# Causal attention on one core: scores are centred and transposed before the exponential, and rows are divided per token

## The chip, the cores and the metric

The kernel runs on one core of one Trainium2 chip. The metric is the device time of one execution in microseconds (us): 4361.49 us, median of 3 runs (4361.11 to 4366.51). Engines: PE is TensorE (matmuls and transposes), DVE VectorE, ACT ScalarE, POOL GpSimd, SP the engine that issues the DMAs.

## The reference, cut to what matters

Three kinds of layer follow each other over 8 batches of 512 tokens by 256 features. The change touches only the last attention, "attention b":

```python
qkv = x @ w_qkv + b_qkv                     # 16 heads of 16
dot = einsum('bhid,bhjd->bhij', q, k)
vals = q_norm_sq + k_norm_sq.T
scores = dot * dot / (vals - 2.0 * dot + 1e-6)
scores = scores + triu(ones, k=1) * -1e9     # causal
attn = softmax(scores, axis=-1)
out = einsum('bhij,bhjd->bhid', attn, v)
return out @ w_out + b_out
```

Everything is float32. The batches are worked through in two groups of four; in each group attention a, a feed-forward block x, attention b and a feed-forward block y follow each other, so attention b stands twice in the program.

## The kernel before, in words

**Units and steps.** In attention b a batch is cut into four row blocks of 128 queries, i = 0 to 3; block i sees 128(i+1) keys. A unit is what fits into two PSUM banks: 2 x 4 heads of 128 keys for i = 0, 2 x 2 heads of 256 for i = 1, 2 x 1 heads of 384 for i = 2 (768 columns in all), 2 x 1 heads of 512 for i = 3 (1024 columns, as for i = 0 and 1). So a batch has 2 + 4 + 8 + 8 = 22 units and a group 88. The two halves of a unit are called a = 0 and a = 1. `steps` runs a software pipeline by hand: in step s, unit s gets its denominators, unit s-1 its squares, unit s-2 its maximum, unit s-3 is transposed, and in odd steps units s-5 and s-4 are multiplied with the values. `order_keeper` ties every instruction of an engine to the one issued before it on that engine, so the order in which the parts stand in `each_part` is the order on each engine; engines meet only by semaphores.

**What a unit does.** `product` makes den (the denominator, 18 rows) and, a step later, dot (16 rows) on PE, line L1312; the matmuls of den(s) and dot(s-1) take turns. `inverse` is a logarithm and an exponential on ACT (both recorded under the helper's line L241, tile r). `error` (L1331, tile t, reads den and r) and `refine` (L1335) improve 1/den on DVE. `squares` (L1341) squares dot on ACT into num, ahead of `inverse` in the step where the unit has several heads in a half (i = 0 and 1), after it otherwise. `masked` (L1347) adds the mask on POOL. `highest` (L1354) multiplies num by r and keeps each head's row maximum, one DVE instruction for a head; POOL negates it (L1364). `exponentials` (L241, num from num) is one ACT instruction for a head, with the maximum as bias and the row sum as a second output. `turn` (L1384) transposes one half, block by block of 128, into the single PSUM buffer of pool `ps_mm`; `keep_turned` (L1389) copies it to SBUF on DVE. `values` (L1399) multiplies with v.

**Buffers.** Pool `ps_s` has three PSUM buffers of two banks and is used by den, dot and one piece per step; `ps_mm` and `ps_o` (the sums over values) have one each.

**Pieces.** Work beside the units is cut into pieces with up to five parts (`first`, `act`, `second`, `dve`, `late`) that `each_part` puts at fixed places of a step. `stacks_and_values` gives the 11 pieces that prepare the next batch: one transpose, eight side pieces (called heavy: two matmuls `pu`, a square on ACT `sq` (L1210), a matmul with `sel_b` as the part `second` (L1213), an eviction on DVE (L1226) or ACT (L1232)), and two value pieces `pv`. `project` gives two pieces per row block, that divide and project the finished rows. `a_piece` chooses one piece for a step: projections first where the step is odd or their number is even, then a preparing piece, but no heavy one in an odd step beyond the fourth; if there is none, an idle matmul `kept_awake` (L1289). What is left of the preparation when the next batch begins is run by `whole`, part after part, ahead of that step:

```python
if step % each == 0:
    with kept_order():
        while prologues or norms:
            whole((norms or prologues).popleft())
```

Of the kernel before, what the change touches and what calls it, by code (L numbers as in the profile page):

```python
# [11 lines left out]
F32 = mybir.dt.float32  # L12
# [28 lines left out]
Unit = namedtuple("Unit", "n product inverse error refine masks squares masked highest exponentials turn keep_turned values project")  # L41
# [5 lines left out]
def kernel(  # L47
# [14 lines left out]
    b_wo,  # L62
    f_wqkv,
# [108 lines left out]
    def weights_b(name):  # L172
        flat = wts.tile([P, 4096], F32, tag="wa", name=f"wb_{name}", bufs=2)
        wl, at = part(flat, 0, (2, INNER))
        wr, at = part(flat, at, (2, INNER))
        wv, at = part(flat, at, (2, D))
        wo, at = part(flat, at, (4, D))
        bv, at = part(flat, at, (D,))
        for s, d in ((b_wl, wl), (b_wr, wr), (b_wv, wv), (b_wo, wo)):
            fetch(s, d)  # L180
        fetch(b_bv, bv, False)
        return wl, wr, wv, wo, bv
# [991 lines left out]
    def attention_b(batches, g, norms_b, state):  # L1174
        wl_b, wr_b, wv_b, wo_b, bv_b = weights_b(g)

        def stacks_and_values(b):
# [72 lines left out]
            def value_piece(t2):  # L1250
# [13 lines left out]
                def keep_values():  # L1264
                    if t2 == 0:
                        state[b]["v"] = pool.tile([P, NT, (HB + 1) * HDB], F32, tag="v", name=f"v_b{b}")
                        nc.gpsimd.memset(state[b]["v"][:, :, HB * HDB :], 1.0)
                    pv = got.pop("pv")
                    for i in range(2):
                        nc.vector.tensor_add(state[b]["v"][:, 2 * t2 + i, : HB * HDB], pv[:, i, 0], bv_b)  # L1270
# [22 lines left out]
        def unit(b, i, qp, js, first, last):  # L1293
# [55 lines left out]
            def highest(num, r):  # L1349
# [14 lines left out]
                nc.gpsimd.tensor_scalar(most[:, 8 : 8 + nh], most[:, :nh], -1.0, 0.0, ALU.mult, ALU.add)  # L1364
                return most

            def exponentials(num, most):
                if first:
                    state["sums"] = pool.tile([P, HB], F32, tag="sumsb", name=f"sums_{n}")
                sums, s4 = state["sums"], per_head(num)  # L1370
                for at, (a, m, h) in enumerate(heads):
                    function(
                        s4[:, a, m, :],
                        s4[:, a, m, :],
                        AF.Exp,
                        bias=most[:, 8 + at : 9 + at],
                        accum_out=sums[:, h : h + 1],
                    )
                return sums

            def turn(p, a):
                ppt = ps_mm.tile([P, NT, P], F32, tag="mm", name=f"ppt_{n}_{a}")
                for k in range(cols // P):
                    nc.tensor.transpose(ppt[:, k, :], p[:, a, k * P : (k + 1) * P], ident)  # L1384
                return ppt

            def keep_turned(ppt, pt, a):
                nblocks = cols // P
                nc.vector.tensor_copy(pt[:, a, :nblocks, :], ppt[:, :nblocks, :])  # L1389

            def values(pt):
# [3 lines left out]
                v = state[b]["v"]  # L1395

                def one(m, j, k, a):
# [3 lines left out]
                        lhsT=v[:, k, (4 * j + q) * HDB : (4 * j + q + 2) * HDB],  # L1401
# [12 lines left out]
            def project(sums):  # L1414
# [5 lines left out]
                nc.vector.reciprocal(sums, sums)  # L1420

                def turned():
                    prt = ps_s.tile([P, 2, 4, P], F32, tag="s", name=f"prt_{n}")
                    for k in range(4):
                        for q in range(4):
                            one = sums[:, 4 * k + q : 4 * k + q + 1].to_broadcast([P, 32])
                            nc.tensor.matmul(
                                prt[q * 32 : (q + 1) * 32, 0, k, :], lhsT=one, rhs=ident, start=True, stop=True
                            )
                    kept_awake(prt)  # L1430
                    got["prt"] = prt[:, 0]

                def kept():
                    got["rt"] = pool.tile([P, 4, P], F32, tag="two", name=f"rt_{n}", bufs=7)
                    nc.scalar.copy(got["rt"], got.pop("prt"))

                def divided():
                    got["oT"] = pool.tile([P, 4, P], F32, tag="two", name=f"oT_{n}", bufs=7)
                    nc.vector.tensor_mul(got["oT"], state["o"], got.pop("rt"))

                def projected():
                    got["pp"] = ps_s.tile([P, 2, T], F32, tag="s", name=f"pp_{n}")[:, 0, :D]
                    for k in range(4):
                        nc.tensor.matmul(
                            got["pp"], lhsT=got["oT"][:, k, :], rhs=wo_b[:, k, :], start=(k == 0), stop=(k == 3)
                        )

                def added():
                    nc.vector.tensor_add(xs[b][:, i, :], got.pop("pp"), xs[b][:, i, :])

                return [Piece(False, turned, kept, None, divided), Piece(False, projected, None, None, added)]

            return Unit(n, product, inverse, error, refine, len(js), squares, masked, highest, exponentials, turn, keep_turned, values, project)
# [9 lines left out]
        def steps(ahead):  # L1463
# [6 lines left out]
            den, dot, r, t, num, most, sums, ppt, pt = ({} for _ in range(9))  # L1470
# [18 lines left out]
            def each_part(s):  # L1489
# [5 lines left out]
                with_values = s % 2 == 1 and unit_of(5) is not None  # L1495
                if with_values:
                    for u in (s - 5, s - 4):
                        projections.extend(units[u].project(sums.pop(u)))
                piece = a_piece(s) if s >= EARLY_STEPS else Piece(False)
# [4 lines left out]

                products = []
# [8 lines left out]
                if unit_of(3):  # L1514
                    pt[s - 3] = pool.tile([P, 2, NT, P], F32, tag="pt", name=f"pt_{units[s - 3].n}", bufs=3)
                    turned = units[s - 3].turn(num[s - 3], 0)
                do(piece.first)
                if with_values:
                    in_turns(*[units[u].values(pt.pop(u)) for u in (s - 5, s - 4)])
                if unit_of(1):  # L1520
                    units[s - 1].refine(t.pop(s - 1), r[s - 1])

# [3 lines left out]
                if unit_of(0):  # L1526
                    r[s] = units[s].inverse(den[s])
                do(piece.act)
                if unit_of(1) and not first:
                    num[s - 1] = units[s - 1].squares(dot.pop(s - 1))  # L1530
                if unit_of(2):
                    most[s - 2] = units[s - 2].highest(num[s - 2], r.pop(s - 2))
                if unit_of(1):
                    units[s - 1].masked(num[s - 1])
                if unit_of(3):
                    units[s - 3].keep_turned(turned, pt[s - 3], 0)
                    turned = units[s - 3].turn(num.pop(s - 3), 1)
                do(piece.second)
                if unit_of(2):
                    sums[s - 2] = units[s - 2].exponentials(num[s - 2], most.pop(s - 2))  # L1540
                if unit_of(0):
                    t[s] = units[s].error(den.pop(s), r[s])
                if unit_of(3):
                    units[s - 3].keep_turned(turned, pt[s - 3], 1)
# [96 lines left out]
def laid_out(inputs):  # L1641
# [18 lines left out]
    wo_b = np.zeros((HB, 2, HDB, D), f)  # L1660
    wo_b[:, 0] = i["L0_attn_b_w_out"].reshape(HB, HDB, D)
    wo_b[HB - 1, 1, 0] = i["L0_attn_b_b_out"]

# [4 lines left out]
    for half, rest in ((0, 0), (1, GATES)):  # L1668
# [19 lines left out]
        "b_wo": wo_b.reshape(INNER, D),  # L1688
# [28 lines left out]
```

## Time and profile before

| | |
|---|---|
| median of 3 runs | 4361.49 us |
| the profiled execution | 4372.94 us, of which 4371.1 us from the first to the last instruction |
| mean granted TensorE clock | 0.991 |
| attention b, first and last `error` (L1331) of group 0 | 1013.9 to 1471.6 us |
| the same of group 1 | 3184.2 to 3642.3 us |

All durations below come from this one profiled execution; it is 0.26% above the median. Busy shares on the page are of the whole span, and attention b holds about a fifth of it, so its rows have to be read by stretch.

### The profile page before, as it was taken

To read this page: it belongs to the slowest core of one execution; us is meant where nothing else is said; L and a number is where in the kernel's file an instruction comes from. 1 tells how busy PE (TensorE), PEld (TensorE's weight loads), DVE (VectorE), ACT (ScalarE), POOL (GpSimd) and SP (SyncE) were. 2 spreads that over 40 slices of the span, in tenths; PEclk is the share of its full clock that TensorE was granted. 3 is DMA by queue.
4 is the path that set the end of the run, shared out by engine and by line. 5 is a ranking of instruction groups with operands and counts; after the bars stand their busy time and mean duration, and the time that the engine had idled before them with its cause. 6 is when DMAs were issued, how large, how long until landed. Compare 5 with 4: busy or idle time off the path is not lost.

```text
span 4371.1 us, 70487 instructions
## 1 busy us (share of the span) xinstructions
PE 4122.6 (94%) x26580; PEld 2578.8 (59%) x26580; DVE 3069.1 (70%) x7505; ACT 2686.5 (61%) x6316; POOL 1144.6 (26%) x1140
## 2 busy tenths in 40 slices
PE   8999999999998899999999999999999988999999
PEld 5666656655555466566566666566555554665665
DVE  6678737746999887377466786477379997864773
ACT  6777517616989675276167775276179896752761
POOL 0014314312222343143200242143122223422431
PEclk9999999999999999999999999999999999999999
DMA  2000000000000000000100000000000000000000
GB/s 83 1 23 4 23 3 23 3 25 21 2 1 1 20 4 7 3 23 14 53 30 1 20 4 24 23 3 24 5 21 1 1 1 20 4 6 23 3 4 24
DMA packets 51091, 63.36 MB, mean 14 GB/s; under 512 B 6336, under 2 KB 45504, under 8 KB 50752
## 3 DMA queue, kind: packets, MB, share of 16 engines
q1 hardware_dynamic: 50752, 58.85, 4.1%
q8 instruction: 211, 3.46, 0.3%
q14 instruction: 128, 1.05, 0.1%
HBM read 46.28 MB, written 4.19 MB: 12 GB/s over the span
## 4 chain that ended last, share of the span: by engine, by line
PE 67%; DVE 21%; ACT 10%; issue 1%; POOL 1%; DMA 0%; SPq 0%; POOLq 0%; ACTq 0%; DVEq 0%
PE pu_g1x L1042 3%; PE pu_g0y L1042 3%; PE pu_g1y L1042 3%; PE pu_g0x L1042 3%; PE s_a L393 3%; PE o_a L429 3%; PE ppt_a L418 3%; ACT r_b L241 2%; PE pqk_f1x L514 2%; PE pqk_f0x L514 2%; PE pqk_f1y L514 2%; PE pqk_f0y L514 2%; DVE pt_b L1389 2%; PE ppt_b L1384 2%; ACT num_b L241 2%; DVE r_b L1335 2%
## 5 line engine op out<-in xcount | busy, mean ns | idle before, releaser
L1384 PE MATMUL ppt_b<-ident,num_b 128*128 128x128 f32 x1280 | 223.5, 291 | 88.0 <-DVE pt_b L1389 65.3
L1384 PEld LDWEIGHTS ppt_b<-ident,num_b 128*128 128x128 f32 x1280 | 137.6, 143 | 273.4 <-ACT num_b L241 98.7
L241 ACT ACTIVATE num_b<-num_b,most_b 128x512 f32<-128x512 f32 (+3 forms) x512 | 280.7, 552 | 22.0 <-POOL most_b L1364 21.7
L1389 DVE COPY pt_b<-ppt_b 128x512 f32<-128x512 f32 (+1 forms) x352 | 224.3, 637 | 28.5 <-PE ppt_b L1384 27.8
L241 ACT ACTIVATE p_a<-s_a,nm_a 128x512 f32<-128x512 f32 x256 | 173.5, 682 | 105.1 <-DVE nm_a L397 101.9
L1331 DVE TENSOR_TENSOR t_b<-den_b,r_b 128x1024 f32<-128x1024 f32 (+1 forms) x176 | 197.5, 1122 | 45.4 <-ACT r_b L241 44.9
L1354 DVE CUSTOM_DVE_ANT_0 num_b<-num_b,r_b 128x512 f32<-128x512 f32 (+3 forms) x512 | 226.2, 490 | 1.9 <-POOL num_b L1347 1.9
L1347 POOL TENSOR_TENSOR num_b<-num_b,causal 128x256 f32<-128x256 f32 (+2 forms) x176 | 174.0, 988 | 186.3 <-ACT num_b L1341 185.7
L1312 PE MATMUL den_b<-st_b,st_b 18*128 18x384 f32 (+3 forms) x1024 | 208.5, 472 | 0.4 <-ACT num_b L1341 0.4
L397 DVE TENSOR_REDUCE nm_a<-s_a 128x2 f32<-128x1024 f32 x128 | 156.4, 1223 | 70.6 <-PE s_a L393 70.6
L1335 DVE SCALAR_TENSOR_TENSOR r_b<-t_b,r_b 128x1024 f32<-128x1024 f32 (+1 forms) x176 | 204.9, 1164 | 0.2
L1312 PE MATMUL dot_b<-st_b,st_b 16*128 16x384 f32 (+3 forms) x1024 | 189.6, 472 | 6.2 <-ACT yT_b L1190 4.4
L411 ACT ACTIVATE p_a<-p_a,sums_a 128x512 f32<-128x512 f32 x256 | 171.9, 720 | 26.5 <-DVE sums_a L409 26.5
L241 ACT ACTIVATE r_b<-den_b 128x1024 f32<-128x1024 f32 (+1 forms) x176 | 165.7, 941 | 35.1 <-PE den_b L1312 17.5
L241 ACT ACTIVATE p_f0y<-p_f0y,nm_f0y,rn_f0y 128x256 f32<-128x256 f32 (+1 forms) x256 | 143.7, 563 | 63.2 <-DVE nm_f0y L653 63.2
L1341 ACT ACTIVATE num_b<-dot_b 128x1024 f32<-128x1024 f32 (+1 forms) x176 | 164.6, 935 | 28.3 <-PE dot_b L1312 28.3
L241 ACT ACTIVATE p_f1y<-p_f1y,nm_f1y,rn_f1y 128x256 f32<-128x256 f32 (+1 forms) x256 | 143.7, 564 | 61.3 <-DVE nm_f1y L653 61.3
L1364 POOL TENSOR_SCALAR most_b<-most_b 128x2 f32<-128x2 f32 (+2 forms) x176 | 34.0, 193 | 557.1 <-DVE most_b L1354 541.8
L241 ACT ACTIVATE p_f0x<-p_f0x,nm_f0x,rn_f0x 128x256 f32<-128x256 f32 (+1 forms) x256 | 143.7, 563 | 57.7 <-DVE nm_f0x L653 57.7
L241 ACT ACTIVATE p_f1x<-p_f1x,nm_f1x,rn_f1x 128x256 f32<-128x256 f32 (+1 forms) x256 | 143.7, 564 | 56.3 <-DVE nm_f1x L653 56.3
L241 ACT ACTIVATE r_b<-r_b 128x1024 f32<-128x1024 f32 (+1 forms) x176 | 172.4, 980 | 5.6
L556 POOL TENSOR_TENSOR ro_f1x<-ro_f1x,rs_f1x 128x512 f32<-128x512 f32 x64 | 80.2, 1274 | 355.5 <-DVE sums_f1x L726 182.0
(356 smaller groups left out, 11230.4 us busy)
## 6 DMA issues: line engine op xcount, KB each, us to landing
x<-in_x SPq DMA_DIRECT2D x8, 512.0 KB
out<-x SPq DMA_DIRECT2D x8, 512.0 KB
wf_0x<-in_f_wqkv SPq DMA_DIRECT2D x2, 1536.0 KB
wf_0y<-in_f_wqkv SPq DMA_DIRECT2D x2, 1536.0 KB
wf_1x<-in_f_wqkv SPq DMA_DIRECT2D x2, 1536.0 KB
wf_1y<-in_f_wqkv SPq DMA_DIRECT2D x2, 1536.0 KB
wg_0x<-in_f_w SPq DMA_DIRECT2D x2, 1386.0 KB
wg_0y<-in_f_w SPq DMA_DIRECT2D x2, 1386.0 KB
```

The lines of the kernel that those rows point to most:

```text
L241: i = nc.scalar.activation(out, in_, func, **more).ins
L411: nc.scalar.activation(p[:, odd], p[:, odd], AF.Identity, scale=some[:, odd : odd + 1])
L514: nc.tensor.matmul(dst.rearrange("p h d -> p (h d)"), lhsT=hTs[b][:, k, t * P : (t + 1) * P], rhs=wqkv[:, k, c * INNER : (c + 1) * INNER], ...
L1042: nc.tensor.matmul(pu[: cols.stop - cols.start, c], lhsT=w1[:, k, cols], rhs=hT[:, k, :], start=(k == 0), stop=(k == 1),)
L1312: return nc.tensor.matmul(s[:, a, m * width : (m + 1) * width], lhsT=left[at, j, past:width], rhs=right[at, j, :width], start=True, stop=True,
L1331: nc.vector.tensor_mul(t[:, :, :cols], den[:, :, :cols], r[:, :, :cols])
L1335: nc.vector.scalar_tensor_tensor(r[:, :, :cols], t[:, :, :cols], 2.0, r[:, :, :cols], ALU.subtract, ALU.mult)
L1341: nc.scalar.activation(num[:, :, :cols], dot[:, :, :cols], AF.Square, scale=-0.5)
L1347: nc.gpsimd.tensor_add(own, own, mask)
L1354: nc.vector.tensor_tensor_reduce(out=s4[:, a, m, :], in0=s4[:, a, m, :], in1=r4[:, a, m, :], scale=-1.0, scalar=LOWEST, op0=ALU.mult, op1= ...
L1384: nc.tensor.transpose(ppt[:, k, :], p[:, a, k * P : (k + 1) * P], ident)
L1389: nc.vector.tensor_copy(pt[:, a, :nblocks, :], ppt[:, :nblocks, :])
```

## The change

Exponentials are taken after the transpose instead of before it. In a step, `centred` now subtracts the row maximum on DVE (for i = 2 and 3 one subtraction of a per-row scalar for each half, for i = 0 and 1 one subtraction of a broadcast tile for each half); `turn` transposes the centred scores; `exponentials` is one ACT instruction for each half, reads the transposed PSUM bank and writes SBUF. The negation on POOL, the exponentials per head and the DVE copies are gone. The values carry a column of ones behind each head's 16 columns, so that the row sums come out of `values` as a 17th row of each head. `project` now copies the result from PSUM, transposes it back to tokens (four transposes), takes the reciprocal of the sums and multiplies on DVE, transposes the 256 columns back (two transposes), copies them, and projects them with two matmuls and one for the bias; before, 16 matmuls spread the reciprocals over the rows, with an idle matmul, a copy, a product on DVE and four matmuls. The bias of the projection is a tile of its own, loaded by a DMA of its own.

The places in the step change too: half 0 is transposed first of all on PE, ahead of den and dot; half 1 follows the piece's first part; `values` come after it; `centred` stands behind `error` on DVE; new projections are put in line after the step's piece has been chosen, not before it.

```diff
-                nc.gpsimd.tensor_scalar(most[:, 8 : 8 + nh], most[:, :nh], -1.0, 0.0, ALU.mult, ALU.add)
                 return most
-            def exponentials(num, most):
...
+            def centred(num, most):
+                s4 = per_head(num)
+                if len(js) > 1:
+                    nh = len(heads)
+                    m = most[:, :nh].rearrange("p (m a) -> p a m", a=2)
+                    for a in range(2):
+                        nc.vector.tensor_sub(
+                            s4[:, a], s4[:, a], m[:, a].unsqueeze(2).to_broadcast([P, len(js), width])
+                        )
+                    return
                 for at, (a, m, h) in enumerate(heads):
+                    nc.vector.tensor_scalar(
+                        s4[:, a, m, :], s4[:, a, m, :], most[:, at : at + 1], None, ALU.subtract
                     )
...
-            def keep_turned(ppt, pt, a):
+            def exponentials(ppt, pt, a):
                 nblocks = cols // P
-                nc.vector.tensor_copy(pt[:, a, :nblocks, :], ppt[:, :nblocks, :])
+                function(pt[:, a, :nblocks, :], ppt[:, :nblocks, :], AF.Exp)
...
-                        lhsT=v[:, k, (4 * j + q) * HDB : (4 * j + q + 2) * HDB],
+                        lhsT=v[:, k, (4 * j + q) * (HDB + 1) :][:, : 2 * HDB],
...
+                def kept():
+                    got["o"] = pool.tile([P, 4, P], F32, tag="two", name=f"ob_{n}", bufs=7)
+                    nc.scalar.copy(got["o"], state["o"])
                 def turned():
+                    got["po"] = ps_s.tile([P, 2, 4, P], F32, tag="s", name=f"po_{n}")[:, 0]
+                    o = got.pop("o")
                     for k in range(4):
-                        for q in range(4):
-                            one = sums[:, 4 * k + q : 4 * k + q + 1].to_broadcast([P, 32])
-                            nc.tensor.matmul(
-                                prt[q * 32 : (q + 1) * 32, 0, k, :], lhsT=one, rhs=ident, start=True, stop=True
-                            )
-                    kept_awake(prt)
+                        nc.tensor.transpose(got["po"][:, k, :], o[:, k, :], ident)
...
+                return [Piece(False, None, kept, turned, divided), Piece(False, returned, columns, projected, added)]
...
                 with_values = s % 2 == 1 and unit_of(5) is not None
+                piece = a_piece(s) if s >= EARLY_STEPS else Piece(False)
                 if with_values:
                     for u in (s - 5, s - 4):
-                        projections.extend(units[u].project(sums.pop(u)))
-                piece = a_piece(s) if s >= EARLY_STEPS else Piece(False)
+                        projections.extend(units[u].project())
...
+                if unit_of(3):
+                    pt[s - 3] = pool.tile([P, 2, NT, P], F32, tag="pt", name=f"pt_{units[s - 3].n}", bufs=3)
+                    turned = units[s - 3].turn(num[s - 3], 0)
+                    units[s - 3].exponentials(turned, pt[s - 3], 0)
...
-                if unit_of(3):
-                    pt[s - 3] = pool.tile([P, 2, NT, P], F32, tag="pt", name=f"pt_{units[s - 3].n}", bufs=3)
-                    turned = units[s - 3].turn(num[s - 3], 0)
                 do(piece.first)
-                if with_values:
-                    in_turns(*[units[u].values(pt.pop(u)) for u in (s - 5, s - 4)])
...
+                if unit_of(3):
+                    turned = units[s - 3].turn(num.pop(s - 3), 1)
+                    units[s - 3].exponentials(turned, pt[s - 3], 1)
+                if with_values:
+                    in_turns(*[units[u].values(pt.pop(u)) for u in (s - 5, s - 4)])
                 do(piece.act)
...
-                if unit_of(3):
-                    units[s - 3].keep_turned(turned, pt[s - 3], 0)
-                    turned = units[s - 3].turn(num.pop(s - 3), 1)
-                do(piece.second)
-                if unit_of(2):
-                    sums[s - 2] = units[s - 2].exponentials(num[s - 2], most.pop(s - 2))
                 if unit_of(0):
                     t[s] = units[s].error(den.pop(s), r[s])
-                if unit_of(3):
-                    units[s - 3].keep_turned(turned, pt[s - 3], 1)
+                if unit_of(2):
+                    units[s - 2].centred(num[s - 2], most)
+                do(piece.second)
                 do(piece.dve)
                 do(piece.late)
```

## The prediction

> **What bounds the kernel now.** I read the page's busy table first, then windows cut at the starts of `error` (L1331, one per step) of each batch, then the timeline of single steps, then the groups by form. The page:
>
> ```profile
> span 4371.1 us, 70487 instructions
> ...
> PE 4122.6 (94%) x26580; PEld 2578.8 (59%) x26580; DVE 3069.1 (70%) x7505; ACT 2686.5 (61%) x6316; POOL 1144.6 (26%) x1140
> ```
>
> That is an average over stages with other limits. The windows of attention b's second, third and last batch of group 0 and of one short stretch (columns: stretch, length, busy us and instructions of PE, PEld, DVE, ACT, POOL, granted clock, DMA share, GB/s):
>
> ```profile
> 1136.40:1252.30 115.90, 105.95 (x982) 60.05 (x982) 107.18 (x237) 106.07 (x213) 25.62 (x45) 0.99 0.01 1
> 1252.30:1369.00 116.70, 107.87 (x976) 60.40 (x976) 107.27 (x238) 105.42 (x212) 25.60 (x45) 0.97 0.01 1
> 1369.00:1475.10 106.10, 88.92 (x914) 50.61 (x914) 102.86 (x239) 95.66 (x197) 27.25 (x47) 0.98 0.01 1
> 1242.60:1246.00 3.40, 3.40 (x11) 2.84 (x11) 3.40 (x7) 3.37 (x4) 0.56 (x2) 0.50 0.00 0
> ```
>
> DVE is busy 92% of a middle batch, ACT 90 to 92%, PE 91 to 92%. A batch has 22 steps, 5.3 us each. From one start of L1331 to the next, the trace gives by row block of the unit: i=0 5.67 us, i=1 5.95, i=2 4.67, i=3 5.26. One i=3 step in the timeline, from `error` to the next `error` (columns: start, length, engine, line, operation, tiles):
>
> ```profile
> 1444.21 1.21 DVE L1331 TENSOR_TENSOR t_b<-den_b,r_b 128x1024 f32<-128x1024 f32 x1
> ...
> 1444.89 0.69 PE L1312 MATMUL den_b<-st_b,st_b 18*128 18x512 f32 x1
> ...
> 1445.34 0.55 DVE L1389 COPY pt_b<-ppt_b 128x384 f32<-128x384 f32 x1
> ...
> 1446.11 1.01 ACT L241 ACTIVATE r_b<-den_b 128x1024 f32<-128x1024 f32 x1
> ...
> 1447.15 1.06 ACT L241 ACTIVATE r_b<-r_b 128x1024 f32<-128x1024 f32 x1
> ...
> 1448.26 0.69 DVE L1389 COPY pt_b<-ppt_b 128x512 f32<-128x512 f32 x1
> ...
> 1448.87 1.22 DVE L1331 TENSOR_TENSOR t_b<-den_b,r_b 128x1024 f32<-128x1024 f32 x1
> ```
>
> 4.66 us. `den` starts 0.68 us after `error` begins, before `error` has even ended: PE isn't held by DVE. den to logarithm takes 1.22, logarithm to the exponential's end 2.10 (1446.11 to 1448.21), and then r waits 0.66 us for DVE. So DVE's own queue (error 1.13, copy 0.47, reciprocal 0.16, refine 1.08, highest 1.21, copy 0.61, from start to start) sets a step that has no heavy piece; the chain den, logarithm, exponential, error has 0.66 us to spare.
>
> **The change, part by part.** The prices (columns: count, busy us, mean ns, idle before):
>
> ```profile
> L1389 DVE COPY pt_b<-ppt_b 128x512 f32<-128x512 f32 x224 | 153.7, 686 | 16.8 <-PE ppt_b L1384 16.1
> L1439 DVE TENSOR_TENSOR oT_b<-o_b,rt_b 128x512 f32<-128x512 f32 x32 | 21.8, 682 | 6.7 <-PE o_b L1399 6.7
> L287 DVE TENSOR_SCALAR yr_b<-x,mv_b,rstd_b 128x256 f32<-128x256 f32 x32 | 11.0, 407 | 2.8 <-POOL rstd_b L267 2.8
> L241 ACT ACTIVATE num_b<-num_b,most_b 128x128 f32<-128x128 f32 x128 | 49.5, 390 | 0.7 <-POOL most_b L1364 0.7
> L1435 ACT COPY rt_b<-prt_b 128x512 f32<-128x512 f32 x32 | 18.6, 580 | 19.3 <-PE prt_b L1289 19.1
> ```
>
> *Work.* The per-row subtraction has no row; L287 is nearest (scalars per row, SBUF to SBUF): 340 ns at 128 columns, 407 at 256, so 0.474 us at 384, 0.54 at 512; bounds 0.41 (the 256-column row) and 0.69 (the copy, if the fast rate is lost). The broadcast subtraction is nearest to L1439, 0.68; bounds 0.54 and 0.81 (the eviction L1226). From start to start DVE saves about 0.15 x 2 in an i=3 step, 0.08 x 2 in i=2, nothing for i=0 and 1. On ACT, exponentials with their accumulator reads cost from start to start 8 x 0.385 = 3.1 us (i=0), 4 x 0.49 = 2.0 (i=1), 2 x 0.60 (i=2), 2 x 0.71 (i=3); two reads of PSUM like L1435 cost 2 x 0.48, or 2 x 0.39 at 384. ACT saves 0.4 to 2.1 us a step. POOL's negation (193 ns) leaves. On throughput alone the change gains.
>
> *Order.* But half 0's transposes now stand on PE ahead of den(s+1), and they wait for the first subtraction of unit s-2, which stands on DVE behind error(s). Queued behind that wait on PE: den and dot, for which the logarithm on ACT waits, for which error(s+1) waits. That closes a loop of one step:
>
> error(s) start to start 1.13 (0.865 at 768 columns) + first subtraction 0.54 (0.47 for i=2, 0.68 for i=0, 1) + DVE to PE 0.1 (0.05 to 0.15 in the timeline) + four transposes up to den 0.57 (three: 0.45) + den to logarithm 1.2 (0.98) + logarithm, exponential and start of error 2.15 (1.72).
>
> i=3: 5.69 us. i=2: 4.59. Where the former unit has several heads its squares (0.90) stand ahead of the logarithm: i=1 6.74, i=0 6.59. DVE's new sum, 4.4 for i=3, is below that, so the loop replaces DVE as the limit. By step of a batch (err of s, subtraction of s-2, products of s+1): 2 x 6.59 + 3 x 6.74 + 6.31 + 2 x 4.93 + 5 x 4.59 + 5.24 + 2 x 5.50 + 6 x 5.69 = 122.9 us.
>
> *Heavy pieces.* Their selector matmul (L1213) is the last on PE in a step; it waits for `sq`, now behind exponential a=1: 0.49 + 0.69 + 0.07 after error begins, and takes 1.0, so PE is free at 2.25 us (2.14 for i=2) where the transposes would start at 1.77 (i=3), 1.44 (i=2), 1.91 (i=0, 1). Penalty 0.48, 0.70, 0.34 us. The order of the changed program has six in-step heavy pieces in middle batches: 0.34 + 2 x 0.70 + 3 x 0.48 = 3.2 us.
>
> *Displaced pieces.* In that order, projections take an even and an odd step each (before, they often took two odd ones), so preparation no longer fits in 22 steps. Two heavy and both value pieces run in a heap at the end of middle batches, one heavy and both value pieces at the end of the first: on PE 0.9 + wait 0.85 + 1.0 for a heavy one, 0.86 for a value piece. The heap starts 0.45 us after error (when values are done) and PE is free at 7.75 instead of 1.77 us: +6.0; in the first batch +3.2.
>
> *Hidden.* Projection's six transposes, copies, reciprocal and product: `second` of its first piece ends about 1.6 us after error, level with the wait. It would cost 0.3 us x 32 if it came later. The bias DMA is in the stage's load, issued long before use. The memset of ones (0.15 us, POOL 22% busy) is free.
>
> *Sum.* Middle batches: 122.9 + 3.2 + 6.0 = 132.1 against 116.6 on average, +15.5, four times. Last batch: 21 steps, 122.9 - 5.7 = 117.2 against 106.1, +11.1, twice. First batch: its first three steps (4.5, 10.1, 6.9 us) have nothing to transpose; the rest is 103.0 + 3.5 + 3.2 = 109.7 against 101, +9, twice. Together +102 us.
>
> *Clock.* In the fourth window above, the granted clock is 0.50 for 3.4 us, and means of 0.97 to 0.99 say that a batch has one or two such dips. In the new step PE waits 1.3 us more, and projection steps lose their idle matmul. One more dip in a batch halves PE's 1.77 us in the loop once or less: I take 0.75 us x 8 = 6. [...]
>
> 102 + 6 = 108 us: the profiled execution would go from 4372.94 to 4481 us, the median from 4361.5 to 4469.5.
>
> **Rivals.**
> 1. *Throughput decides (faster).* DVE and ACT are over 90% busy; if the subtraction is seen by PE within the 0.68 us after error's start at which den starts now, the loop is slack and DVE's sum rules: 64 x 0.30 + 64 x 0.16 for i=3 and 2, and for i=1 and 0, which ACT's exponentials hold at about 6 us, down to DVE's 4.84: about 32 x 1.0 + 16 x 0.3. -66 us: 4295. For it: the busy shares. Against: error alone takes 1.13 us, and the subtraction is behind it. Chance 0.07.
> 2. *The clock goes (much slower).* More idle PE, dips in most steps: +108 + 60 to 130, 4530 to 4600. For it: dips exist already. Against: PE still works in every 3.4 us. Chance 0.13.
> 3. *Gain and loss cancel.* If semaphores and PE's start cost 0.25 us less per step than I sum, +65; it would have to be 0.6 us to reach zero. No change, within 0.2% (some 9 us, about what a measurement of this kernel can tell): chance 0.02.
>
> **How the numbers follow.** Loop with heap as summed: 0.78. Its own range: 0.25 us a step either way (170 steps, 43 us); subtraction without the fast rate, 0.15 us x 128 = 19; heap 36 us give or take half. That gives 4415 to 4530; to leave out less than 2 in 10 the upper end goes into rival 2: 4550, the lower to 4405. Slower 0.91, faster 0.07.
>
> **What would show it.** Right: starts of `error` 5.7 us apart for i=3 and 6.7 for i=1; PE idle ahead of half 0's transposes, put down to the subtraction, 1.3 us a step, some 200 us in all where now 88.0; DVE idle ahead of `error` for ACT's r, some 150 us; middle batches of 132 us with `pu` and `pv` in a row at their end. Wrong: den starting less than 1.5 us after `error`; DVE still over 90% busy; a granted clock below 0.95 in attention b (rival 2).

## The result and the profile after

The changed kernel takes 4627.96 us, median of 4 runs (4621.6 to 4629.88), beside 4364.0 us (4361.11 to 4373.17) for the kernel before on the same chip: ratio 1.0599, 95% interval 1.0579 to 1.0618. That is 264 us slower. The forecast was slower by 108, in a range that ended at 4550: the direction was right, the size was not. The profiled execution took 4621.6 us, 248.7 more than the profiled one of before, and the traces account for that: attention b, from its first `error` to its last, grew from 457.7 to 582.3 us in group 0 and from 458.05 to 580.25 in group 1, together +247. (The profiled run of before lies 9 us above its median, that of the changed kernel 6 below its own; hence 248.7 beside 264.)

The page after (the lines that answer to those of before, and the granted clock in 40 slices):

```profile
span 4619.8 us, 67995 instructions
...
PE 4204.3 (91%) x25668; PEld 2644.3 (57%) x25668; DVE 3058.1 (66%) x7505; ACT 2601.6 (56%) x5676; POOL 1131.1 (24%) x972
...
PEclk9999999998888899999999999999988888999999
```

DVE's and ACT's work fell by 11 and 85 us, as the change says, and the span grew. The clock line has two troughs, and they are the two stages of attention b. The four batches of group 0 (columns: stretch, length, busy us and instructions of PE, PEld, DVE, ACT, POOL, granted clock, DMA share, GB/s):

```profile
1014.40:1161.70 147.30, 117.17 (x792) 70.09 (x792) 109.83 (x239) 90.63 (x125) 26.90 (x27) 0.84 0.05 16
1161.70:1312.10 150.40, 117.25 (x870) 68.99 (x870) 105.31 (x236) 95.02 (x132) 25.24 (x24) 0.85 0.00 1
1312.10:1463.00 150.90, 118.24 (x864) 69.26 (x864) 105.49 (x236) 95.02 (x132) 24.79 (x24) 0.84 0.00 1
1463.00:1596.80 133.80, 97.42 (x748) 57.58 (x749) 99.73 (x233) 82.08 (x114) 25.02 (x25) 0.78 0.00 1
```

In a middle batch DVE is now busy 70% of the time (92% before), ACT 63%, PE 78%, and PE's 78% is stretched by a clock of 0.84: from one `pu` record to the next 0.43 us pass at clock 1 and 0.85 at 0.5. No engine is full, so waits set the time. The two groups that carry them (columns: count, busy us, mean ns, idle before, and what ended it):

```profile
L1392 PE MATMUL ppt_b<-ident,num_b 128*128 128x128 f32 x1280 | 242.1, 316 | 123.0 <-DVE num_b L1385 84.7
L1339 DVE TENSOR_TENSOR t_b<-den_b,r_b 128x1024 f32<-128x1024 f32 (+1 forms) x176 | 198.4, 1127 | 215.9 <-ACT r_b L244 215.6
```

PE waits for the subtraction (L1385; with the broadcast one, L1380, 118 us), DVE waits for the reciprocal r. PE has a second wait of this size, for ACT's copy of the value sums (`ob_b`) ahead of a projection's first transposes (columns: total us, times, longest):

```profile
PE ppt_b L1392 <- DVE num_b L1385: 84.7, 54, 3.5
PE po_b L1437 <- ACT ob_b L1431: 83.8, 32, 3.6
```

An i=3 step without a heavy piece, from `error` to the next `error`:

```profile
1271.51 1.23 DVE L1339 TENSOR_TENSOR t_b<-den_b,r_b 128x1024 f32<-128x1024 f32 x1 [0.50 <-ACT r_b L244]
...
1272.65 1.35 DVE L1385 TENSOR_SCALAR num_b<-num_b,most_b 128x512 f32<-128x512 f32 x2
...
1273.28 0.63 PE L1392 MATMUL ppt_b<-ident,num_b 128*128 128x128 f32 x4 [1.67 <-DVE num_b L1385]
...
1273.84 0.69 PE L1320 MATMUL den_b<-st_b,st_b 18*128 18x512 f32 x1
...
1275.03 1.02 ACT L244 ACTIVATE r_b<-den_b 128x1024 f32<-128x1024 f32 x1 [0.49 <-PE den_b L1320]
...
1276.08 1.06 ACT L244 ACTIVATE r_b<-r_b 128x1024 f32<-128x1024 f32 x1
...
1277.17 1.23 DVE L1339 TENSOR_TENSOR t_b<-den_b,r_b 128x1024 f32<-128x1024 f32 x1 [0.81 <-ACT r_b L244]
```

It is the loop of the forecast, link by link: error 1.14, subtraction to transposes 0.63, transposes to den 0.56, den to logarithm 1.19, logarithm and exponential to the next error 2.14. Together 5.66 us, where 5.69 was summed; den starts 2.33 us after `error`, 0.68 before. PE sits idle for 1.67 us of it.

The heap at the end of a middle batch, one step of 15.01 us:

```profile
1297.10 1.23 DVE L1339 TENSOR_TENSOR t_b<-den_b,r_b 128x1024 f32<-128x1024 f32 x1 [1.17 <-ACT r_b L244]
1297.34 1.98 PE L1203 MATMUL pu_b<-yT_b,wb 128*128 128x512 f32 x4
...
1300.10 1.13 PE L1216 MATMUL pu_b<-sq_b,sel_b 128*128 128x512 f32 x2 [0.78 <-ACT sq_b L1213]
...
1301.07 1.88 PE L1203 MATMUL pu_b<-yT_b,wb 128*128 128x512 f32 x4
...
1304.69 3.62 PE L1259 MATMUL pv_b<-wb,yT_b 128*128 128x256 f32 x16
...
1308.14 0.60 PE L1392 MATMUL ppt_b<-ident,num_b 128*128 128x128 f32 x4
```

Half 0's transposes start 11.04 us after `error`, not 7.75 as forecast. The two `pu` matmuls of a piece are four records of 0.43 us, and the two value pieces sixteen of 0.22: the forecast had taken one record for one matmul.

### The profile page after: what moved, and what is told of

The parts are those of the page before. It is cut to its first block, busy times and chain, and to the rows that moved or that the text cites. A ratio compares the mean times of both kernels' runs of the same rounds, so it can differ in the third digit from the quotient of the medians.

```text
span 4619.8 us, 67995 instructions
## 1 busy us (share of the span) xinstructions
PE 4204.3 (91%) x25668; PEld 2644.3 (57%) x25668; DVE 3058.1 (66%) x7505; ACT 2601.6 (56%) x5676; POOL 1131.1 (24%) x972
## 4 chain that ended last, share of the span: by engine, by line
PE 71%; DVE 16%; ACT 11%; issue 1%; POOL 1%; DMA 0%; SPq 0%; POOLq 0%; ACTq 0%; DVEq 0%
ACT r_b L244 4%; PE den_b L1320 4%; PE pu_g1x L1045 3%; PE pu_g0y L1045 3%; PE pu_g1y L1045 3%; PE pu_g0x L1045 3%; PE ppt_b L1392 3%; PE s_a L396 3%; PE o_a L432 3%; PE ppt_a L421 3%; PE pu_b L1203 2%; PE pqk_f0x L517 2%; PE pqk_f1x L517 2%; PE pqk_f1y L517 2%; PE pqk_f0y L517 2%; DVE t_b L1339 2%
## 5 line engine op out<-in xcount | busy, mean ns | idle before, releaser
L1355 POOL TENSOR_TENSOR num_b<-num_b,causal 128x256 f32<-128x256 f32 (+2 forms) x176 | 190.6, 1083 | 993.5 <-ACT num_b L1349 888.5
L1392 PE MATMUL ppt_b<-ident,num_b 128*128 128x128 f32 x1280 | 242.1, 316 | 123.0 <-DVE num_b L1385 84.7
L244 ACT ACTIVATE pt_b<-ppt_b 128x512 f32<-128x512 f32 (+1 forms) x352 | 194.1, 552 | 283.4 <-PE ppt_b L1392 279.6
L1339 DVE TENSOR_TENSOR t_b<-den_b,r_b 128x1024 f32<-128x1024 f32 (+1 forms) x176 | 198.4, 1127 | 215.9 <-ACT r_b L244 215.6
L1392 PEld LDWEIGHTS ppt_b<-ident,num_b 128*128 128x128 f32 x1280 | 183.2, 164 | 259.2 <-issue 137.8
L1320 PE MATMUL dot_b<-st_b,st_b 16*128 16x384 f32 (+3 forms) x1024 | 226.7, 550 | 0.0
L1320 PE MATMUL den_b<-st_b,st_b 18*128 18x384 f32 (+3 forms) x1024 | 226.1, 550 | 0.0
L559 POOL TENSOR_TENSOR ro_f0x<-ro_f0x,rs_f0x 128x512 f32<-128x512 f32 x64 | 80.3, 1275 | 355.4 <-DVE sums_f0x L729 186.2
L421 PEld LDWEIGHTS ppt_a<-ident,p_a 128*128 128x128 f32 x1024 | 110.2, 141 | 95.1 <-ACT p_a L244 43.2
```

The lines of the kernel that those rows point to most:

```text
L244: i = nc.scalar.activation(out, in_, func, **more).ins
L421: nc.tensor.transpose(ppt[:, odd, k, :], p[:, odd, k * P : (k + 1) * P], ident)
L1320: return nc.tensor.matmul(s[:, a, m * width : (m + 1) * width], lhsT=left[at, j, past:width], rhs=right[at, j, :width], start=True, stop=True,
L1339: nc.vector.tensor_mul(t[:, :, :cols], den[:, :, :cols], r[:, :, :cols])
L1355: nc.gpsimd.tensor_add(own, own, mask)
L1392: nc.tensor.transpose(ppt[:, k, :], s[:, a, k * P : (k + 1) * P], ident)
```

## The experiments

In the traces the clock is 1 or 0.5. "Time at half rate" is the time at 0.5 inside the steps of attention b, both groups, in the one profiled execution: 51 us in the kernel before, 388 in the changed one (61 and 403 in the expectations, from an earlier count). Each ratio is to runs of the kernel before beside that kernel on the same chip; their medians lie between 4364.0 and 4371.6 us. The step means are over all eight batches; the forecast's 5.67 and 5.95 us for i=0 and 1 leave out the first batch of each group.

| Kernel | Median us | Ratio to before, 95% | Half rate us | Mean step i=0, 1, 2, 3 us |
|---|---|---|---|---|
| before | 4364.0 | 1 | 51 | 5.97, 6.10, 4.67, 5.26 |
| after | 4627.96 | 1.0599 [1.0579, 1.0618] | 388 | 7.00, 7.71, 5.67, 7.11 |
| `awake` | 4577.2 | 1.0472 [1.0453, 1.0490] | 245 | 6.69, 7.53, 5.33, 7.09 |
| `awake_t` | 4585.8 | 1.0498 [1.0475, 1.0521] | 211 | 6.96, 7.27, 5.33, 6.95 |
| `centred_first` | 4542.8 | 1.0392 [1.0376, 1.0407] | 303 | 7.35, 6.98, 5.21, 6.56 |
| `pieces_first` | 4574.5 | 1.0456 [1.0435, 1.0478] | 323 | 7.05, 7.70, 5.74, 6.25 |
| `three` | 4467.5 | 1.0223 [1.0207, 1.0239] | 106 | 7.15, 7.17, 5.08, 5.56 |
| `four` | 4429.85 | 1.0138 [1.0118, 1.0158] | 64 | 7.26, 6.60, 4.78, 5.39 |
| `four_nomask` | 4392.8 | 1.0054 [1.0034, 1.0074] | 38 | 6.10, 6.10, 4.94, 5.32 |
| `prod_first` | 4646.4 | 1.0623 [1.0603, 1.0644] | 436 | 7.14, 7.55, 5.90, 7.31 |
| `division_only` | 4379.95 | 1.0015 [1.0006, 1.0024] | 130 | 5.74, 6.09, 4.84, 5.23 |
| `division_awake` | 4365.78 | 0.9987 [0.9976, 0.9997] | 27 | 5.81, 5.84, 4.80, 5.21 |
| `before_no_idle` | 4361.4 | 0.9983 [0.9970, 0.9996] | 48 | 5.73, 6.06, 4.57, 5.20 |

### Keeping PE busy in the projection (`awake`)

```diff
+                def idle():
+                    got["po"] = ps_s.tile([P, 2, 4, P], F32, tag="s", name=f"po_{n}")
+                    kept_awake(got["po"])
...
+                    kept_awake(got["ps"].rearrange("p a b (c d) -> p a (b c) d", d=P))
...
-                return [Piece(False, None, kept, turned, divided), Piece(False, returned, columns, projected, added)]
+                return [Piece(False, idle, kept, turned, divided), Piece(False, returned, columns, projected, added)]
```

> The changed kernel with one idle matmul added to each of the two projection pieces, in the part that stands between the products and the second half's transposes; nothing else moves. Clock theory (the 403 us at half rate in attention b, against 61 before, come from projection steps in which only transposes follow the products): half-rate time falls below 120 us, middle batches from 150 to about 136 us, 4628 falls by about 100 to 4530. Loop theory alone (the step is set by error, subtraction, transposes, products, logarithm, exponential; the clock is a side matter): no more than 15 us change, 4615 to 4640, since the idle matmul lies beside the loop. Work theory (there is simply more to do): slightly slower.

51 us saved by adding work to PE: the clock does cost time, and about half of what the clock theory said. The two profiled executions (4621.6 and 4584.69 us) differ by 36.9 us for 143 us less at half rate, 0.26 us for each; the mean granted clock of all four runs of each, 0.953 and 0.974, gives the same with the medians (the last expectation below has 0.32). Steps that had been at half rate fell to the loop's lengths (the eleventh of the last batch from 5.99 to 4.58), but 245 us stayed, some 110 of them still in steps of a projection.

### The subtraction ahead of `error` (`centred_first`)

```diff
-                if unit_of(0):
-                    t[s] = units[s].error(den.pop(s), r[s])
                 if unit_of(2):
                     units[s - 2].centred(num[s - 2], most)
+                if unit_of(0):
+                    t[s] = units[s].error(den.pop(s), r[s])
```

> The changed kernel with the subtraction put ahead of error on DVE instead of behind it; nothing else moves. Loop theory: error (1.13 us) and the subtraction (0.54) leave the path to the next step's transposes; the loop becomes error, release of den's buffer, products, logarithm, exponential: 4.7 us for i=3 (5.66 now), 3.7 for i=2 (4.58), 5.6 for i=1 (6.74). About 21 us a batch, 8 batches: -170 us, to 4460, if the clock stays as it is. Clock theory alone, or work theory: within 30 us of 4628.

85 us saved. The light steps fell: i=3 from 5.66 to 4.98 us, i=2 from 4.58 to 4.20 in the middle batches and to 3.70 in the last, where the loop had said 4.7 and 3.7. The timeline of that i=3 step, lines of DVE and PE:

```profile
1253.91 0.48 DVE L1385 TENSOR_SCALAR num_b<-num_b,most_b 128x512 f32<-128x512 f32 x1
1254.30 1.22 DVE L1339 TENSOR_TENSOR t_b<-den_b,r_b 128x1024 f32<-128x1024 f32 x1
1254.59 0.66 PE L1392 MATMUL ppt_b<-ident,num_b 128*128 128x128 f32 x4 [0.42 <-ACT pt_b L244]
1255.18 0.69 PE L1320 MATMUL den_b<-st_b,st_b 18*128 18x512 f32 x1
```

Den starts 0.88 us after `error` instead of 2.33, and DVE has no idle time ahead of `error` in this step. What is missing to the expected 4460 sits in heavy steps, which stayed at 5.7 to 6.0, in i=0 steps, which got longer (7.00 to 7.35; a likely cause is under `three`), in the heaps, and in 303 us at half rate.

### The pieces in the old order (`pieces_first`)

```diff
-                piece = a_piece(s) if s >= EARLY_STEPS else Piece(False)
                 if with_values:
                     for u in (s - 5, s - 4):
                         projections.extend(units[u].project())
+                piece = a_piece(s) if s >= EARLY_STEPS else Piece(False)
```

> The changed kernel with new projections put in line before the step's piece is chosen, as in the kernel before. The heaps at the ends of the batches (steps of 15.0 and 11.4 us where 5.7 is usual: 4 x 9.3 + 2 x 5.7 = 49 us) should vanish; two heavy pieces more stand inside the steps (0.6 us each, 8 us in all). Heap theory: -40 us, 4588. If the preparation only costs the same elsewhere: within 10 us of 4628.

The heap went (its steps fell from 15.01 and 11.39 to 5.77 us) and 53 us with it, 14 more than expected. Why it is more isn't shown: time at half rate fell by 65 us as well.

### The three together (`three`)

The three diffs above in one kernel.

> All three edits together: idle matmuls in the projection pieces, subtraction ahead of error, projections in line first. If the three causes add (100 + 170 + 40): about 4320, which would be faster than the kernel before by 1%. If clock and loop overlap (PE works more densely in a shorter step anyway, so the clock's share shrinks): 4340 to 4400. If one of the causes was misjudged: above 4430.

One by one the edits saved 51 + 85 + 53 = 189 us, together 160, and the result lies above the 4430 from which the text called something misjudged. The timeline of `three` shows a wait that none of the theories held, DVE and POOL in the first two steps of a batch:

```profile
1279.15 2.82 POOL L1355 TENSOR_TENSOR num_b<-num_b,causal 128x1024 f32<-128x1024 f32 x1 [0.73 <-ACT num_b L1349]
...
1279.68 2.97 DVE L1385 TENSOR_SCALAR num_b<-num_b,most_b 128x512 f32<-128x512 f32 x2
...
1286.15 2.36 POOL L1355 TENSOR_TENSOR num_b<-num_b,causal 128x1024 f32<-128x1024 f32 x1 [4.18 <-ACT num_b L1349]
1286.23 2.43 DVE L1362 CUSTOM_DVE_ANT_0 num_b<-num_b,r_b 128x128 f32<-128x128 f32 x1
```

A subtraction of 512 columns takes 0.48 us as a rule, and the first of the two here 2.58 (in the i=3 step of the changed kernel above one is held too, which makes the two 1.35); a `highest` of 128 columns takes 0.29 elsewhere and 2.43 here. Each time POOL's mask addition began first, and the DVE instruction ends just behind it (0.29 and 0.15 us). So a longer record isn't more work, but a wait that the profile counts as busy. Summed over the 69 such records of `three`, each beside an instruction of POOL, what exceeds the median of the same form is about 71 us (75 in an expectation below). The same count gives 11 us in the kernel before, 37 in the changed one and 70 in `centred_first`: the repaired order makes the two engines meet.

### The heavy piece's square ahead of half 1's exponential (`four`)

```diff
-                    units[s - 3].exponentials(turned, pt[s - 3], 1)
...
                 do(piece.act)
+                if unit_of(3):
+                    units[s - 3].exponentials(turned, pt[s - 3], 1)
```

> The kernel with the three edits, and with the piece's ACT part (the square of a heavy piece, the copies of a projection) ahead of the second half's exponential instead of behind it. Heavy theory (the steps with a heavy piece, 5.7 to 6.2 us, are set by the square, the selector matmul behind it, and the transposes behind that): the square starts up to 0.5 us sooner, so 48 heavy steps lose 0.5 us each: -24 us, to about 4443. If heavy steps are set by PE's two projection matmuls instead (four records of 0.43 us), the square isn't what is late: 4460 to 4475.

38 us less than `three`; heavy i=2 steps fell from 5.9 to 5.3 us. Much of the heavy piece's penalty came from where its square stood on ACT. The edit moves a projection's copies too (PE's wait for `ob_b` goes from 37.9 to 28.6 us); what each is worth isn't told apart.

### The same without the mask (`four_nomask`)

```diff
-                if unit_of(1):
-                    units[s - 1].masked(num[s - 1])
```

> The kernel with the four edits, without the causal mask (POOL's 176 additions of the mask are left out, so the sums run over all keys of the unit). Port theory (a DVE instruction with two SBUF inputs, or the fast subtraction, that meets a POOL addition waits for its end: in the run with three edits such instructions take 75 us longer than their medians): those holds vanish, and 40 to 75 us of the time with them. If these long records are only how overlaps are drawn: within 10 us of the kernel with four edits.

37 us less, just under the expected 40 to 75. i=0 steps, whose mask addition is the longest, fell from 7.26 to 6.10 us. The lengthened records are gone (2 us by the count above, 78 in `four`), so POOL's instruction was their cause, and about half of their time lay on the path. (Without POOL's instruction its wait for the squares goes too; the two aren't told apart. How the one engine holds the other isn't shown.)

### Transposes in place of the idle matmuls (`awake_t`)

Against `awake`, at both of its places:

```diff
+        def turned_idle(space):
+            for k in range(8):
+                nc.tensor.transpose(space[:, 1, k % 4, :], ident, ident)
...
-                    kept_awake(got["po"])
+                    turned_idle(got["po"])
```

> As the run with idle matmuls in the projection pieces of the changed kernel, but with eight 128 x 128 transposes (0.9 us) in place of each idle matmul (two passes of 0.43 to 0.5 us): the same time on PE, of the other kind. If transposes don't count as activity for the clock: half-rate time stays near 400 us, 4628 or a little more. If any PE work counts: half-rate time near 245 us and 4577, as with the idle matmuls.

4585.8 us, ratio 1.0498 (1.0475 to 1.0521), 211 us at half rate. The transposes kept the clock up about as well as the matmuls (245 us); over all four runs of each the mean granted clock is 0.972 and 0.974, and 0.953 with neither. The second batch of group 0, `awake`, then `awake_t`; the number ahead of the DMA share is the clock, 0.85 for this batch of the changed kernel:

```profile
1157.80:1297.04 139.24, 110.35 (x886) 62.74 (x886) 106.53 (x236) 95.21 (x132) 25.50 (x24) 0.96 0.00 1
```

```profile
1157.65:1298.89 141.24, 113.23 (x934) 70.38 (x934) 105.75 (x236) 95.19 (x132) 24.67 (x24) 0.94 0.00 1
```

Of the two outcomes that the expectation names, it is the second: here a transpose kept the clock as a matmul did. The trace of the changed kernel agrees: in 113 windows of 3.41 us (see below) PE was busy 0.7 or more of the time, but under 0.6 without its transposes, and the clock stayed up after every one.

### The kernel before without its idle matmuls behind the spreading (`before_no_idle`)

```diff
-                    kept_awake(prt)
```

> The kernel before, without the 32 idle matmuls behind the 16 matmuls that spread the reciprocals. Clock theory: some of the windows around projections now lack activity, half-rate time rises from 61 us towards 100 to 160, +10 to +35 us. If the spreading matmuls and the shorter steps keep the clock by themselves: no change or a few us faster, since PE has 1.0 us less to do in 32 steps.

Ratio 0.9983 (0.9970 to 0.9996), 48 us at half rate in the profiled execution. But over all ten runs the mean granted clock is 0.989, against 0.992 for the 15 runs of the kernel before beside them, or some 28 us more at half rate. So these 32 idle matmuls did keep the clock up a little, and the kernel is no slower without them all the same. Its ratio is the lowest of the study, not clear of that of `division_awake`.

### Den and dot ahead of the transposes (`prod_first`)

```diff
-                if unit_of(3):
-                    pt[s - 3] = pool.tile([P, 2, NT, P], F32, tag="pt", name=f"pt_{units[s - 3].n}", bufs=3)
-                    turned = units[s - 3].turn(num[s - 3], 0)
-                    units[s - 3].exponentials(turned, pt[s - 3], 0)
...
                     in_turns(*products)
+                if unit_of(3):
+                    pt[s - 3] = pool.tile([P, 2, NT, P], F32, tag="pt", name=f"pt_{units[s - 3].n}", bufs=3)
+                    turned = units[s - 3].turn(num[s - 3], 0)
+                    units[s - 3].exponentials(turned, pt[s - 3], 0)
```

> The changed kernel with den and dot ahead of half 0's transposes on PE, as they stood before; on ACT half 0's exponential still stands ahead of the logarithm. Loop theory: the products leave the loop, but the logarithm now waits behind the exponential that waits for the transposes: error 1.13, subtraction 0.54, 0.1, transposes to the end of the last 0.73, exponential 0.49, logarithm to error 2.15: 5.14 us for steps of i=3 without a piece (5.66 in the changed kernel), 4.17 for i=2 (4.58). Steps with a heavy piece gain nothing, since the selector matmul stands ahead of the products. In all -20 to -60 us. If the order on PE doesn't matter: the light steps stay at 5.66 and 4.58.

Missed: 4646.4 us, ratio 1.0623 (1.0603 to 1.0644), 436 us at half rate, and the light steps unchanged (i=3 5.67, i=2 4.55). The timeline says why:

```profile
1277.03 1.23 DVE L1339 TENSOR_TENSOR t_b<-den_b,r_b 128x1024 f32<-128x1024 f32 x1 [1.12 <-ACT r_b L244]
...
1278.31 0.69 PE L1320 MATMUL dot_b<-st_b,st_b 16*128 16x512 f32 x1 [0.77 <-DVE t_b L1339]
...
1279.38 0.66 PE L1392 MATMUL ppt_b<-ident,num_b 128*128 128x128 f32 x4
...
1280.56 1.02 ACT L244 ACTIVATE r_b<-den_b 128x1024 f32<-128x1024 f32 x1
```

The products now wait for `error` itself (`t_b`), which reads den in PSUM, and `ps_s` has three buffers for den, dot and the piece; and ACT's half-0 exponential stands ahead of the logarithm and waits for transposes that come later. So a second loop of the same length stands behind the first; it is read from this timeline, no run tests it.

### The division alone (`division_only`), and with idle matmuls (`division_awake`)

`division_only` is the kernel before with the ones column, the division by token and the new projection as in the change; exponentials (without their row sums) and order stay as before. `division_awake` adds to it the idle matmuls of `awake`, by the same diff.

```diff
-                        nc.vector.tensor_add(state[b]["v"][:, 2 * t2 + i, : HB * HDB], pv[:, i, 0], bv_b)
+                        nc.vector.tensor_add(
+                            state[b]["v"][:, 2 * t2 + i, :HB, :HDB],
...
-                        accum_out=sums[:, h : h + 1],
...
-            def project(sums):
+            def project():
```

> The kernel before with one part of the change alone: a column of ones beside the values, division by token, the new projection and its bias, and no row sums from the exponentials; exponentials, transposes, DVE copies and the order of the steps stay as before. If the loss comes from where the exponentials stand and from the order (loop, heaps, clock in the longer steps): this part alone costs nothing, and may gain, since ACT has 512 accumulator reads (0.093 us each, 48 us) less, of which the steps of i=0 and 1 are bound by ACT: 16 x 0.74 + 32 x 0.37 = 24 us; 4340 to 4370. If the new projection (more steps of its chain, transposes in place of the idle matmul) is what costs: 4390 to 4430, with more half-rate time.

> This is the kernel before with the ones column, the division by token and the new projection alone (4379.95 us, 130 us at half rate), and an idle matmul in both projection pieces. If its loss is the clock in the projection steps, the time at half rate goes back to about 50 us, and at 0.32 us of time for a microsecond at half rate (what the idle matmuls saved in the changed kernel) 80 us less give 25 us: about 4355, at or a little below the kernel before. If the projection's own work on the engines is what costs, the time stays at 4380, and two more matmuls of 0.9 us in 16 steps each can only add, up to 4395.

The division costs 0.15% by itself: the steps are a little shorter or the same but for i=2 (4.67 to 4.84), and time at half rate goes from 51 to 130 us. With PE kept busy that time falls to 27 us and the kernel gains 0.13%; by the ratios the 103 us are worth 12 us, half of what was expected, so the price of a microsecond at half rate isn't one number. Why it differs isn't shown; it may hang on whether PE is on the path of the step. So of the two parts of the change the division costs next to nothing, and by difference the 6% are in the other: the exponential behind the transpose, with the order that goes with it.

## Why the prediction was wrong in size

**Right: the loop.** Light steps without half rate measured 5.66 (i=3, summed 5.69), 4.57 to 4.58 (4.59), 5.22 (5.24), 5.48 (5.50), 6.92 to 6.99 (6.74, i=1) and 6.70 to 6.74 (6.59, i=0). DVE waits 215.6 us for r, where "some 150" was said, and `centred_first` broke the loop as it should. PE's wait for the subtractions is 118 us, not "some 200". Rival 1 is out: DVE and ACT were far from full.

**Wrong: the clock.** "One more dip in a batch halves PE's 1.77 us in the loop once or less: I take 0.75 us x 8 = 6." That is the step that failed: the time measured for the clock is about 98 us. Steps that no half-rate stretch touches, put in for those that one does, make attention b about 149 us longer than before; the other 98 of the 247 go with the clock. By `awake`'s price, 0.26 us for each of the 337 us more at half rate, it would be 88; both are estimates. Rival 2 named this, and its 60 to 130 us hold it (its sum, 4530 to 4600, was passed too, by the pieces below); it was given 0.13 because "PE still works in every 3.4 us". That the clock would fall only after so long a stretch without work was the author's assumption, and the trace refutes it. All 119 changes of the clock in the changed kernel's trace lie on one grid of 3.413 us, to within 0.001 us. Counting PE's busy share in the windows of that grid (after, all windows that ran at full rate):

| Busy share of the window | Next window full | Next window half |
|---|---|---|
| under 0.4 | 0 | 32 |
| 0.4 to 0.5 | 10 | 10 |
| 0.5 to 0.6 | 20 | 14 |
| 0.6 to 0.7 | 74 | 4 |
| 0.7 and more | 1062 | 0 |

(The grid is fitted to the moments at which the clock changed; moved by 0.05 us, it shifts a few windows between rows.) PE needn't be idle for a whole window: half rate followed 24 of the 54 in which it was busy 0.4 to 0.6 of the time. An i=3 step of 5.66 us has 1.67 us of wait in one piece, which some windows take whole.

The other part of the step's failure is the wait for `ob_b`, shown above: 83.8 us, once in each of the 32 row blocks. The forecast looked at these steps, but not at when their first transposes can start. The copy stands on ACT behind half 1's exponential, and the first transposes of the projection wait for it on PE. "Hidden" held for the length of such a step (4.58 us in `awake`, where the clock stays up), but PE idles meanwhile. Of the 51 windows of attention b after which the clock fell, 28 hold mostly the wait for a subtraction and 21 mostly this one. In `division_only`, with the exponentials in their old place, it comes to 4.1 us. No run takes away this wait alone.

From half rate the clock came back after 4 of 10 windows that were busy 0.8 to 0.9 and after 55 of 86 that were busy over 0.9, and after none of 26 below. The trace of before could have told this: there too all 3 windows of 0.3 to 0.4 were followed by half rate (as were 4 of the 1173 of 0.7 and more, which the share doesn't explain). I had read the dips as rare events, and not looked at the busy share ahead of them, nor at the share that the loop would leave.

**Mis-sized: the pieces, 102 against 149.** The heaps measured 9.3 and 5.7 us over a light step (6.0 and 3.2 forecast), 18 us over 4 + 2 batches, because `pu` takes 4 x 0.43 us and a value piece 8 x 0.22, twice "0.9" and "0.86". Heavy i=2 steps mostly take 5.7 to 5.9 us, not 5.29: some 5 us. "Hidden" was wrong in length for the projection's second piece: its matmuls hold PE in the step below, and half 0's transposes, which would start 1.44 us after `error`, start at 2.06. That step takes 5.18 us instead of 4.59; with about 0.5 us for each of 32 row blocks, 16 us. With 7 us for the last batch, which was held against 106.1 us, a window that ran 3.5 us past its last `error`, that is about the 47 us missing. With the 92 of the clock and the 15 between profiled runs and medians it makes nearly all of the 156 us between 108 and 264.

```profile
1234.95 0.96 DVE L1339 TENSOR_TENSOR t_b<-den_b,r_b 128x768 f32<-128x768 f32 x1 [1.43 <-ACT r_b L244]
...
1235.61 0.70 PE L1458 MATMUL pp_b<-wb,ident 128*128 128x256 f32 x2
...
1236.15 1.03 PE L1460 MATMUL pp_b<-wb,oT_b 128*128 128x256 f32 x4
...
1237.01 0.49 PE L1392 MATMUL ppt_b<-ident,num_b 128*128 128x128 f32 x3
```

**What the change is worth at its best.** With all four repairs it is still 1.38% slower, and 1.5% behind `division_awake`, some 66 us; `division_awake` and `before_no_idle` are the two versions that beat both kernels, the one before by 0.13 and 0.17%. 37 of the 66 us go with the mask, taken out of `four`; `division_awake` keeps it, and has 10 us of lengthened records. The rest, 29 us, isn't settled: `four_nomask` is 0.1 to 0.3 us a step behind `division_awake` in every row block.

## What to carry to other kernels

Ask of every change that makes PE wait what share of PE's time it leaves busy, in stretches as long as the grid on which the clock changes in the trace (3.41 us here): in the changed kernel half rate followed 56 of the 86 windows that were busy less than 0.6, and 4 of the 1140 others. It is paid in PE's work beside the wait, where one `pu` record followed the other after 0.85 us instead of 0.43. A wait that costs the step nothing can cost the clock: 21 of the 51 falls in attention b came after windows that hold mostly the wait for `ob_b`. Before a wait is put at the head of an engine's queue, follow what stands behind it once round the step until it comes back to the wait; such a loop can be summed from the rows of the kernel before, here to 0.25 us and mostly to a few hundredths, but the pieces beside it have to be counted in records, not in calls.

## What the runs showed of the hardware

- The granted clock is 1 or 0.5 in the records of the changed kernel, and all 119 of its changes lie on a grid of 3.413 us, to within 0.001 us. Half rate followed all 32 windows of this grid that ran at full rate with PE busy less than 0.4 of the time, 24 of the 54 with 0.4 to 0.6, and 4 of the 1140 with more. What told the 24 from the other 30 isn't shown.
- From one `pu` record to the next 0.85 us pass at half rate, 0.43 at clock 1 (changed kernel).
- In the trace of the changed kernel 72 DVE instructions that read two tiles from SBUF, or subtract a per-row scalar from SBUF to SBUF, began during a mask addition of POOL. 60 of them took over 0.1 us longer than the median of their form and ended behind the addition; the other 12 began in its last 0.14 us. In `three` a `highest` of 0.29 us became 2.43 and a subtraction of 0.48 us 2.58. Of the 14 `error`s, which read one of their two tiles from PSUM, and the 14 evictions of `pu` from PSUM that began during such an addition in that trace, none took longer.
- The two `pu` matmuls of a piece, float32 and 512 columns each, show as four records, 0.43 us from one to the next at clock 1.
